# The order of the value products in one attention step: all four column tiles together, or two and two

## The chip, the cores and the metric

The kernel runs on one core of one Trainium2 chip. The metric is the device time of one execution in microseconds (us). The kernel before took 3443.28 us, the median of three runs (3435.34, 3443.28 and 3454.9 us).

A core has five engines that run their own instruction streams side by side: TensorE (PE in the profile; its weight loads are shown apart as PEld), VectorE (DVE), ScalarE (ACT), GpSimd (POOL) and SyncE (SP). A product on TensorE has a held operand, which is loaded into the array first, and a moving operand, which is streamed through it. A held operand of 32 columns fills only one of four *column tiles* of the array, called tile 0 to tile 3 here. Which tile it is follows from the 32 output partitions that the product writes: 0-31, 32-63, 64-95 or 96-127.

## What is computed

Sixteen graphs of 1024 nodes with 256 features each pass through two graph layers. Layer 0 is attention with 4 heads of 64 features; layer 1, which this change touches, is attention with 8 heads of 32 features and then an MLP of width 1024. Cut to what matters here, layer 1 is:

```python
normed = layer_norm(x, gamma1, beta1)
qkv = normed.reshape(b_, n_, H, HD).transpose(0, 2, 1, 3)        # H = 8, HD = 32
scores = jnp.einsum('bhqd,bhkd->bhqk', qkv, qkv) * scale
masked = jnp.where(adj_matrix[:, None] > 0, scores, -jnp.inf)
attn = jax.nn.softmax(masked, axis=-1)
out = jnp.einsum('bhqk,bhkd->bhqd', attn, qkv)
x = x + out
...
return x + gelu(layer_norm(x, gamma2, beta2) @ W1 + b1) @ W2 + b2
```

The kernel takes the softmax as exponentials times a 0/1 mask. It sums masked weight times value, and also the masked weights alone, and divides one by the other at the end.

## The kernel before

**Two streams.** Layer 0 of one graph is interleaved with layer 1 of the graph before it. `layer0` (L955) and `layer1` (L973) are generators; the loop at L1023 picks which of them emits its next piece. It picks by a model of the engines' times, `Pace` (L90, with its costs in `cost`, L123, and its due times in `enter`, L151). The order on each engine is the order of emission. The last graph's layer 1 has no layer 0 beside it.

**A step of layer 1.** `attention1` (L722) walks through 32 steps for a graph: 2 halves of 512 queries, 2 groups ("quads") of 4 heads, and 8 blocks of 128 keys. That makes 512 steps in all. In iteration i it emits

- `exponentials` (L740) of step i: four score products on TensorE (`ps<-nT` in the profile, 32 rows each) into four PSUM tiles, and four exponentials on ScalarE into two tiles `p` of two heads each, called ps[0] and ps[1];
- `masked` (L758) of step i-1: two multiplications by the mask on VectorE, ps[0] first and then ps[1] (`p<-p,mask`);
- `products` (L762) of step i-3, since `LAG` is 3 (L782). These are the subject of the change.

**The products of a step.** All write to PSUM and add up over the 8 key blocks.

- *Moved* products, four of them. The two heads of ps[0] are streamed, 512 queries at a time, against held values of 32 columns (`po<-p,v`: "values", tiles 0 and 1). They are streamed again against a held tile whose first column is one (`unit`, L249; `po<-p,unit`: "ones", tiles 2 and 3), which gives the sums of the weights. All four write one PSUM tile, `moved`.
- *Held* pieces, 32 of them. Of the two heads of ps[1], pieces of 32 queries are the held operand and the values with a column of ones (33 columns) are streamed (`po<-v,p`). For each head and each of four blocks of 128 queries, the four pieces go to tiles 0, 1, 2, 3. They write another PSUM tile, `held`.

Operands are float32, and TensorE runs each product as two passes. In the built program the passes of a product stand one after the other, each with its weight load. So a step has 8 moved passes and 64 held passes: two moved passes and 16 held passes on every tile.

Before the change the order is: values on tile 0, ones on tile 2, values on tile 1, ones on tile 3, and then the 32 held pieces with the tile as the innermost loop.

**What comes after.** At the last key block of a quad, `heads_out` (L815) takes over: ScalarE copies `moved` (`oT<-po`), VectorE divides `held` by its sums, TensorE transposes the copy (`acc<-ident,oT`), and VectorE divides that too. After the four quads the MLP follows (`mlp`, L872; `ps<-yT,w_sb` and `po<-w_sb,hid`). Layer 0's attention gives TensorE the groups `acc<-v,p` (L567, L588), and its preparation (L484) gives the groups `acc<-w0e,xT`, `acc<-identb,ak` and `acc<-ident,xk`. All engine instructions that go through `Pace` stand in the profile under line 61, so groups are told apart by their tiles.

Of the kernel before, what the change touches and what calls it, by code (L numbers as in the profile page):

```python
# [39 lines left out]
P = 128  # L40
# [136 lines left out]
def fast_path(  # L177
# [24 lines left out]
    nc = Pace(tc.nc)  # L202
# [5 lines left out]
    HD = D // H1  # L208
    NB = N // P
# [4 lines left out]
    BPH = HALF // P  # L214
    Q = 32
    TILE = 64
    AHEAD = 3
    PAIR = 2
    GB = 2
    QUAD = 4  # L220
# [28 lines left out]
    unit = const.tile([P, Q], F32, name="unit")  # L249
# [26 lines left out]
    at = one.tile([P, 3, PAIR, HO, T], F32, name="v0")  # L276
# [93 lines left out]
    def bank0(shape, dtype=F32):  # L370
        i = min((i for i in range(2) if not banks0[i]["busy"]), key=lambda i: banks0[i]["taken"])
        for chain in banks0[i]["readers"]:
            complete(chain)
        banks0[i].update(readers=[], taken=1 + max(bank["taken"] for bank in banks0))
        return ps_a.tile(shape, dtype, f"acc{i}"), banks0[i]
# [55 lines left out]
    def begin(chain, engine, *needs):  # L431
        for n in needs:
            if not callable(n):
                uses(chain, n.tensor.name)
        chains.append([chain, engine, needs])
# [10 lines left out]
    def advance():  # L446
        for _ in range(2):
            for item in list(chains):
                if item in chains and when(item[2]) <= max(nc.now(), nc.free[item[1]]):
                    run(item)  # L450
# [271 lines left out]
    def attention1(half, mask, rinv, half_done):  # L722

        steps = [(n, quad, jb) for n in range(NH) for quad in range(H1 // QUAD) for jb in range(NB)]

        turn = [0]

        def logits_tile():

            turn[0] = (turn[0] + 1) % 6
            if place[0][0] == B and turn[0] >= QUAD:
                return bank0([P, HALF])[0]
            return ps_s.tile([P, HALF], F32, name="ps")

        def exponentials(n, quad, jb):  # L740
            keys = slice(jb % BPH * P, (jb % BPH + 1) * P)
            of_keys, of_queries = half(jb // BPH)[2], half(n)[2]
            tiles = [logits_tile() for _ in range(QUAD)]

            nc.together(tiles)
            for e in range(QUAD):
                q = slice(e * HD, (e + 1) * HD)
                nc.tensor.matmul(tiles[e], of_keys[q, quad, keys], of_queries[q, quad, :], start=True, stop=True)
            nc.together(tiles)
            ps = []  # L750
            for e in range(0, QUAD, PAIR):
                p = eight.tile([P, PAIR, HALF], F32, name="p")
                for i in range(PAIR):
                    nc.scalar.activation(p[:, i, :], tiles[e + i], AF.Exp, scale=SCALE1)
                ps.append(p)
            return ps

        def masked(n, quad, jb, ps):  # L758
            for p in ps:
                nc.vector.tensor_mul(p, p, mask[n][:, jb, None, :].to_broadcast([P, PAIR, HALF]))  # L760

        def products(quad, jb, ps, moved, held):  # L762
            values = half(jb // BPH)[1][:, jb % BPH, :, :]
            for e in range(PAIR):
                hd = quad * QUAD + e
                for at, v in ((e, values[:, hd, 0:HD]), (PAIR + e, unit)):
                    nc.tensor.matmul(
                        moved[at * Q : (at + 1) * Q, :], v, ps[0][:, e, :], start=jb == 0, stop=jb == NB - 1
                    )
            for e in range(PAIR):  # L770
                hd = quad * QUAD + PAIR + e
                for q in range(BPH):
                    for at in range(0, P, Q):
                        nc.tensor.matmul(
                            held[at : at + Q, q, e, :],
                            ps[1][:, e, q * P + at : q * P + at + Q],
                            values[:, hd, :],
                            start=jb == 0 and e == 0 and q == 0,
                            stop=jb == NB - 1 and e == PAIR - 1 and q == BPH - 1,
                        )  # L780

        LAG = 3  # L782
        ready = {}

        def logits_ready():
            return ps_s.ready("ps", QUAD)

        def outs_ready():
            return ps_o.ready("po", 2)

        for i in range(len(steps) + LAG):
            if i < len(steps):
                ready[i] = exponentials(*steps[i])
                advance()
            if 0 <= i - 1 < len(steps):
                masked(*steps[i - 1], ready[i - 1])
                advance()
            if i < LAG:
                yield 1.0, logits_ready
                continue  # L800
            n, quad, jb = steps[i - LAG]
            if jb == 0:
                moved = ps_o.tile([P, HALF], F32, name="po")
                held = ps_o.tile([P, BPH, PAIR, HD + 1], F32, name="po")
            products(quad, jb, ready.pop(i - LAG), moved, held)
            if jb == NB - 1:
                if quad == 0:
                    o = one.tile([P, BPH, D], F32, name="o0")
                chain = heads_out(n, quad, moved, held, o, rinv)
                begin(chain, "vector", held, moved, o)  # L810
                if quad == H1 // QUAD - 1:
                    half_done(n, o, chain)
            yield (2.5, logits_ready, *ready.get(i - LAG + 1, ()), *([outs_ready] if jb == NB - 1 else []))

    def heads_out(n, quad, moved, held, o, rinv):  # L815

        oT = two.tile([P, HALF], F32, name="oT1")
        nc.scalar.copy(oT, moved)
        of_heads = o.rearrange("p k (h e) -> p k h e", e=HD)
        rinv = rinv[:, n * BPH : (n + 1) * BPH, :]  # L820

        def divide(first, sums, src):
            heads = slice(quad * QUAD + first, quad * QUAD + first + PAIR)
            nc.vector.reciprocal(rinv[:, :, heads], sums)
            nc.vector.tensor_mul(
                of_heads[:, :, heads, :], src, rinv[:, :, heads][:, :, :, None].to_broadcast([P, BPH, PAIR, HD])
            )

        yield "vector", held
        divide(PAIR, held[:, :, :, HD], held[:, :, :, 0:HD])  # L830
        yield "tensor", oT, side_ready
        pt = side_bank([P, BPH, QUAD, Q])
        for q in range(BPH):
            nc.tensor.transpose(
                pt[:, q, :, :].rearrange("p e z -> p (e z)"), oT[:, q * P : (q + 1) * P], ident
            )
        yield "vector", pt
        divide(0, pt[:, :, PAIR:, 0], pt[:, :, 0:PAIR, :])
# [650 lines left out]
```

## Time and profile before

| what | value |
|---|---|
| runs | 3435.34, 3443.28, 3454.9 us; median 3443.28 us |
| profiled execution | span 3453.7 us from the first to the last instruction; it is 1.2 us under the slowest of the three runs, and no other time is listed for it |
| mean granted TensorE clock | 0.980 |
| TensorE (PE) busy | 3312.8 us, 96% of the span |
| weight loads (PEld) busy | 2252.1 us, 65% |
| VectorE (DVE) busy | 2981.3 us, 86% |
| ScalarE (ACT) busy | 1935.6 us, 56% |
| GpSimd (POOL) busy | 418.6 us, 12% |
| moved passes, mean of one | 615 ns (2048 with values, 2048 with ones) |
| held passes, mean of one | 199 ns (32768) |
| mask product of one p tile | 1217 ns (1024) |

How to read it: "busy" is the time in which at least one instruction of the engine was under way. TensorE's products are pipelined. A pass is recorded from its start to a modelled end, and the next may start long before that end, also on the same tile. So the distance between starts tells what a pass costs, not its duration. One graph takes some 210 us: about 110 us of layer 1's attention and about 90 us of its MLP, both mixed with layer 0 of the next graph.

### The profile page before, as it was taken

The numbers are of one execution on the slowest core, as the hardware profiler recorded it, in microseconds if no ns is written. First come the engines' busy times: TensorE is split into PE (matmuls) and PEld (weight loads), VectorE is DVE, ScalarE is ACT, GpSimd is POOL, SyncE is SP. The second block draws the span as 40 slices with busy tenths as digits, with TensorE's granted clock in tenths as the row PEclk, the third lists the DMA queues.
The fourth block names the chain that finished last, engine by engine and source line by source line (L and its number), as shares of the span: only waits on it lengthen the run. The fifth ranks groups of instructions, "written<-read, shape, count | busy, mean of one in ns | idle before, by whom it ended". The sixth has DMA issues, their size and how long they took to land.

```text
span 3453.7 us, 141035 instructions
## 1 busy us (share of the span) xinstructions
PE 3312.8 (96%) x64161; PEld 2252.1 (65%) x64161; DVE 2981.3 (86%) x5262; ACT 1935.6 (56%) x4192; POOL 418.6 (12%) x424
## 2 busy tenths in 40 slices
PE   5899999999999999999999999999999999999998
PEld 4558576675856758576585766757667585775846
DVE  5898898988979898898988989889898898989883
ACT  2563846547375573746637466473654737556373
POOL 1102011010110101101020110101101011010200
PEclk9899999999999999999999999999999999999999
DMA  5211202011020111202112020120201102010000
GB/s 135 51 22 40 44 27 57 15 44 40 28 59 21 42 34 34 56 19 59 22 38 46 24 57 19 41 43 26 59 15 46 38 28 62 18 44 23 23 6 15
DMA packets 95728, 131.30 MB, mean 38 GB/s; under 512 B 10385, under 2 KB 61585, under 8 KB 95121
## 3 DMA queue, kind: packets, MB, share of 16 engines
q1 hardware_dynamic: 75104, 87.58, 8.2%
q0 software_dynamic: 18432, 33.56, 6.6%
q8 instruction: 504, 8.26, 1.0%
q10 hardware_dynamic: 1584, 1.05, 0.1%
q14 instruction: 104, 0.84, 0.1%
HBM read 138.68 MB, written 17.04 MB: 45 GB/s over the span
## 4 chain that ended last, share of the span: by engine, by line
PE 72%; DVE 20%; ACT 5%; issue 2%; DMA 1%; POOL 0%; SPq 0%; POOLq 0%; ACTq 0%; DVEq 0%
PE po L61 28%; PE ps L61 24%; PE acc L61 20%; DVE p L61 15%; ACT p L61 2%; DVE o L61 1%; DVE x L61 1%; ACT sq L61 1%; DVE st L61 1%; DVE z L61 1%; ACT mask L61 1%; ACT hb L61 1%; DVE v L61 0%; ACT z L61 0%; DVE hb L61 0%
## 5 line engine op out<-in xcount | busy, mean ns | idle before, releaser
L61 ACT ACTIVATE p<-ps 128x512 f32<-128x512 f32 x2006 | 1042.2, 616 | 384.1 <-PE ps L61 341.5
L61 DVE TENSOR_TENSOR p<-p,mask 128x1024 f32<-128x1024 f32 x1024 | 1186.6, 1217 | 6.8 <-ACT p L61 6.8
L61 DVE SCALAR_TENSOR_TENSOR p<-cb,dinv,mask 128x512 f32<-128x512 f32 x1024 | 711.0, 744 | 0.1
L61 ACT ACTIVATE hid<-ps,b_sb 128x256 f32<-128x256 f32 x512 | 242.0, 473 | 795.0 <-PE ps L61 794.7
L61 PE MATMUL ps<-nT 32*128 32x512 f32 x4012 | 676.3, 655 | 0.0
L61 PEld LDWEIGHTS po<-v,p 128*32 128x32 f32 x32768 | 396.1, 110 | 333.2 <-issue 288.5
L61 PE MATMUL acc<-v,p 128*64 128x65 f32 x16384 | 562.2, 226 | 31.0 <-DVE p L61 14.3
L61 PEld LDWEIGHTS acc<-v,p 128*64 128x64 f32 x16384 | 515.2, 140 | 112.9 <-issue 59.0
L61 PE MATMUL po<-p,v 128*32 128x512 f32 x2048 | 552.9, 615 | 0.0
L61 PE MATMUL po<-p,unit 128*32 128x512 f32 x2048 | 552.7, 615 | 0.0
L61 PE MATMUL ps<-yT,w_sb 128*128 128x256 f32 x2048 | 489.8, 385 | 0.0
L61 PE MATMUL po<-w_sb,hid 128*128 128x256 f32 x2048 | 474.6, 384 | 0.0
L61 PEld LDWEIGHTS po<-w_sb,hid 128*128 128x128 f32 x2048 | 381.7, 190 | 54.5
L61 PEld LDWEIGHTS ps<-yT,w_sb 128*128 128x128 f32 x2048 | 375.5, 190 | 51.5
L61 PE MATMUL po<-v,p 128*32 128x33 f32 x32768 | 391.4, 199 | 12.4 <-issue 8.5
L61 PEld LDWEIGHTS po<-p,v 128*32 128x32 f32 x2048 | 78.5, 109 | 332.9 <-issue 174.7
L61 PEld LDWEIGHTS ps<-nT 32*128 32x128 f32 x4012 | 220.1, 186 | 98.0 <-issue 41.3
L61 POOL TENSOR_TENSOR r<-v,mhalf 128x1 f32<-128x1 f32 (+1 forms) x192 | 157.6, 831 | 705.7 <-DVE v L61 623.8
L61 DVE TENSOR_TENSOR z<-acc,bias_r 128x256 f32<-128x256 f32 x128 | 54.1, 423 | 181.7 <-ACT hb L61 181.4
L61 PE MATMUL acc<-w0e,xT 128*128 128x264 f32 x512 | 154.1, 425 | 37.2 <-DVE z L61 22.9
L61 POOL DMA_DIRECT2D ak<-in_adj_dram x128 | 69.7, 545 | 971.5 <-PE acc L61 959.0
L61 POOL TENSOR_TENSOR r<-v1s,mhalf 128x4 f32<-128x4 f32 x32 | 61.5, 1922 | 981.1 <-DVE v1s L61 981.1
(111 smaller groups left out, 2818.5 us busy)
## 6 DMA issues: line engine op xcount, KB each, us to landing
ak<-in_adj_dram POOLq DMA_DIRECT2D x128, 256.0 KB, 3.9
cb<-esr SPq DMA_DIRECT2D x64, 512.0 KB
xk<-in_x_dram SPq DMA_DIRECT2D x64, 256.0 KB
xl<-in_x_dram SPq DMA_DIRECT2D x32, 512.0 KB
out_dram<-z SPq DMA_DIRECT2D x128, 128.0 KB
w_sb<-in_L_gnn_W_dram SPq DMA_DIRECT2D x2, 1024.0 KB
esr<-rows SPq DMA_DIRECT2D x64, 4.0 KB
v<-in_L_gnn_a_src_dram SPq DMA_DIRECT2D x2, 320.0 KB
```

The costliest lines, as they stand in the source:

```text
L61: return method(*args, **kwargs)
```

## The change

The two *values* products come first, on tiles 0 and 1. Behind them are the 16 held pieces that belong to tiles 2 and 3. Then come the two *ones* products on tiles 2 and 3, and behind them the 16 held pieces that belong to tiles 0 and 1. The products themselves, their operands, their tiles and their number stay the same. The weight that a held piece adds first (`start`) and last (`stop`) is told by e, q and the key block as before, tile by tile.

```diff
         def products(quad, jb, ps, moved, held):
             values = half(jb // BPH)[1][:, jb % BPH, :, :]
+
+            def move(group, v, e):
+                nc.tensor.matmul(
+                    moved[group * Q : (group + 1) * Q, :], v, ps[0][:, e, :], start=jb == 0, stop=jb == NB - 1
+                )
+
+            def hold(groups):
+                for e in range(PAIR):
+                    hd = quad * QUAD + PAIR + e
+                    for q in range(BPH):
+                        for at in (group * Q for group in groups):
+                            nc.tensor.matmul(
+                                held[at : at + Q, q, e, :],
+                                ps[1][:, e, q * P + at : q * P + at + Q],
+                                values[:, hd, :],
+                                start=jb == 0 and e == 0 and q == 0,
+                                stop=jb == NB - 1 and e == PAIR - 1 and q == BPH - 1,
+                            )
+
             for e in range(PAIR):
-                hd = quad * QUAD + e
-                for at, v in ((e, values[:, hd, 0:HD]), (PAIR + e, unit)):
-                    nc.tensor.matmul(
-                        moved[at * Q : (at + 1) * Q, :], v, ps[0][:, e, :], start=jb == 0, stop=jb == NB - 1
-                    )
+                move(e, values[:, quad * QUAD + e, 0:HD], e)
+            hold((PAIR, PAIR + 1))
             for e in range(PAIR):
-                hd = quad * QUAD + PAIR + e
-                for q in range(BPH):
-                    for at in range(0, P, Q):
-                        nc.tensor.matmul(
...
-                        )
+                move(PAIR + e, unit, e)
+            hold((0, 1))
```

The planner is told of the same products in another order, and it re-plans a little. In the built program, in each of 15 graphs, one set of transposes `acc<-ident,oT` stands ahead of a group of score products instead of behind it. In the MLP's stretch a few groups of `acc<-v,p` and `ps<-yT,w_sb` that stood apart are joined (304 runs of `acc<-v,p` become 289, and 219 runs of `ps<-yT,w_sb` become 204). VectorE's and ScalarE's instructions are the same, with a few neighbours changed in place.

More of the change, by code (lines that the diff above doesn't have):

```diff
@@ L763, in products @@
             values = half(jb // BPH)[1][:, jb % BPH, :, :]
-            for e in range(PAIR):
-                hd = quad * QUAD + e
-                for at, v in ((e, values[:, hd, 0:HD]), (PAIR + e, unit)):
-                    nc.tensor.matmul(
-                        moved[at * Q : (at + 1) * Q, :], v, ps[0][:, e, :], start=jb == 0, stop=jb == NB - 1
-                    )
-            for e in range(PAIR):
-                hd = quad * QUAD + PAIR + e
-                for q in range(BPH):
-                    for at in range(0, P, Q):
-                        nc.tensor.matmul(
[L775 to L779, printed above, removed]
-                        )
+            def move(group, v, e):
[14 more added lines that the diff above has]
+                            )
+            for e in range(PAIR):
+                move(e, values[:, quad * QUAD + e, 0:HD], e)
+            hold((PAIR, PAIR + 1))
+            for e in range(PAIR):
+                move(PAIR + e, unit, e)
+            hold((0, 1))
         LAG = 3
```

## The prediction

> **What bounds the kernel now.** I read the page's busy shares and then its chain of work that ended last. TensorE leads:
>
> ```profile
> PE 3312.8 (96%) x64161; PEld 2252.1 (65%) x64161; DVE 2981.3 (86%) x5262; ACT 1935.6 (56%) x4192; POOL 418.6 (12%) x424
> ...
> PE 72%; DVE 20%; ACT 5%; issue 2%; DMA 1%; POOL 0%; SPq 0%; POOLq 0%; ACTq 0%; DVEq 0%
> ```
>
> The averages mix stages, so I next cut one graph's 210 us into stretches. The columns are the stretch, its length, busy us (and instructions) of PE, PEld, DVE, ACT, POOL, then clock, DMA share and GB/s.
>
> ```profile
> 985.00:1035.00 50.00, 49.92 (x1246) 26.06 (x1244) 38.63 (x44) 41.16 (x95) 2.65 (x5) 1.00 0.33 67
> 1035.00:1085.00 50.00, 48.13 (x1354) 26.83 (x1346) 49.52 (x69) 32.86 (x68) 2.46 (x2) 1.00 0.05 9
> 1085.00:1175.00 90.00, 90.00 (x1289) 77.30 (x1290) 79.13 (x170) 31.39 (x62) 17.36 (x14) 1.00 0.12 34
> ```
>
> The first stretch holds steps 0-15 of layer 1's attention: PE is full and VectorE has 11 us to spare. The second holds steps 16-31: VectorE is busy for 49.5 of 50 us, so a faster PE finds nobody to feed it. The third is the MLP, PE's alone. So PE time saved in steps 0-15 counts, and in steps 16-31 hardly.
>
> Then I read two neighbouring steps' products in PE's timeline (start, length, what, count of passes):
>
> ```profile
> 1500.73 0.62 PE L61 MATMUL po<-p,v 128*32 128x512 f32 x1
> 1500.73 0.62 PE L61 MATMUL po<-p,unit 128*32 128x512 f32 x1
> 1500.74 0.62 PE L61 MATMUL po<-p,v 128*32 128x512 f32 x1
> 1500.75 0.62 PE L61 MATMUL po<-p,unit 128*32 128x512 f32 x1
> 1501.18 0.59 PE L61 MATMUL po<-p,v 128*32 128x512 f32 x1
> ...
> 1501.61 0.73 PE L61 MATMUL po<-v,p 128*32 128x33 f32 x63
> 1502.14 0.59 PE L61 MATMUL po<-p,v 128*32 128x512 f32 x1
> 1502.16 0.20 PE L61 MATMUL po<-v,p 128*32 128x33 f32 x1
> 1502.16 0.61 PE L61 MATMUL po<-p,v 128*32 128x512 f32 x1
> 1502.18 0.61 PE L61 MATMUL po<-p,unit 128*32 128x512 f32 x2
> ```
>
> The four first moved passes start together, the four second passes 0.45 us later, the held pieces 0.43 us after that, and these last some 0.55 us. The median of 512 steps, from the first moved start: second pass 453 ns, first held pass 883, last held pass 1432, next group of products 1559 ns.
>
> **What a tile can give.** If a held pass costs its tile a fixed time, reordering gains nothing; if the four tiles get in each other's way, it gains. The records show both. In the median step the first 24 held starts come in fours every 31-33 ns; from about the 28th on they come in twos every 16.6 ns, which is 33.2 ns per tile. The whole run is 549 ns for 63 steps of the count, 34.9 ns per pass of a tile. The floor is a tile's own. `acc<-v,p` streams 65 columns on two wider tiles and repeats every 58.3 ns per tile, and a second moved pass of 512 columns takes 430 ns. Through these two, a pass costs 0.832 ns per column and about 4 ns more; for 33 columns that is 31.5 ns, just what the first fours show. So of 34.9 ns only 3.4 ns are the crowd's. With two tiles at a time one held pass is needed every 15.8 ns, where the crowded phase delivers one every 8.3 ns, so I take the floor.
>
> **The sum for one step.** Before, every tile has 883 ns of moved passes and 16 held passes; the last starts at 1432 and streams until 1432 + 31.5 = 1463 ns. After, tiles 0 and 1 do values until 883 ns and then 16 x 31.5 = 504 ns of held passes: 1387 ns. Tiles 2 and 3 do held passes first, to about 504 + 20 (the first pass after another tiling takes 453, not 430) = 524 ns, then 2 x 430 of ones: 1384 ns. The work of a tile is the same and the tiles stay balanced: the gain is 1463 - 1387 = **0.075 us per step**, the crowd's share and no more. Its two ends, were nothing else in play, are 0 (the 34.9 ns stay) and 0.075.
>
> This needs PE to let held pieces pass the values' waiting second passes. The trace bears on it. The passes of a product stand one behind the other in the program, yet at 1500.73-1500.75 four first passes start ahead of any second. At 1502.14 the next step's values start before the last held record at 1502.16, and both values ahead of both ones, although a ones product stands between them; so it is in 26 of the 512 steps. A pass whose tile is taken doesn't hold up another tile's. But it is some six passes that overtake here; after the change it is 32.
>
> [...]
>
> **On the path.** Batches here are graphs.
> - Steps 0-15 of 15 graphs: 240 x 0.075 = 18.0 us gained. The last graph runs without layer 0, PE-bound (a step every 2.63 us): 32 x 0.075 = 2.4 us.
> - Steps 16-31 of 15 graphs: up to 240 x 0.075 = 18.0 us, which I take as 0. VectorE's stretch is full and ends the stage; it only begins earlier by what steps 0-15 gain.
> - The plan: 15 pairs of neighbouring groups are joined in the PE-bound MLP. A group of 64 `acc<-v,p` records takes 2.02 us on the chain, one of 96 takes 2.95, so 32 records are 0.93 and 0.16 is fixed; eight passes of `ps<-yT` take 1.92 or 1.73 us, so up to 0.19 is fixed. 15 x 0.35 = 5 us gained (0 to 5). The moved transposes wait for the copy `oT`, which in that place ends 2.59 us after the step's first product, about when PE gets there (1.56 + 1.09 us): 0.
> - `moved` is complete some 0.5 us later. Its copy is ScalarE's (56% busy) and needed by PE 0.95 us or more after its end, where it isn't already waited for. Where it is (two places of a graph, copies held by ScalarE's own queue at 3.2-3.3 us): 0. `p` tiles come free at the same step's end: the exponentials that reuse them wait for score products that stand behind: 0.
>
> **The wait that moves.** Held pieces read ps[1], whose mask product ends 1.14 us after that of ps[0]. Before, they start 0.88 us into the step; now at its beginning, and the ones products queue behind the waiting instruction. Median slack is 3.9 us, but in 36 steps ps[1] is late:
>
> ```profile
> 1712.84 2.35 DVE L61 TENSOR_TENSOR p<-p,mask 128x1024 f32<-128x1024 f32 x2
> ...
> 1714.11 0.62 PE L61 MATMUL po<-p,v 128*32 128x512 f32 x1
> ...
> 1715.24 0.66 PEld L61 LDWEIGHTS po<-v,p 128*32 128x32 f32 x64 [0.98 <-DVE p L61]
> ```
>
> The mask product ends at 1715.19, 1.08 us after the values start. Before, 0.55 us of held pieces follow it; after, 0.50 of pieces and 0.86 of ones. The cost of such a step is its lateness plus 0.055, at most 0.883 us. Over the 22 cases in steps 30 and 31, right ahead of the PE-bound MLP, that sums to 13.3 us, which I count. The 14 cases in step 23 (5.8 us) lie in VectorE's stretch: hidden, 5.8 us if not.
>
> Sum: -18.0 - 2.4 - 5 + 13.3 = **-12 us** against the profiled execution's 3453.7 (0.35%): 3441.6. On the runs' median 3443.28, 0.3% under that execution, it is 3431 us.
>
> **Rivals.**
> 1. *It overlaps, and the late waits are absorbed or steps 16-31 gain as well.* For it: PE waits little there (1.6 us of a graph). Against it: VectorE's 49.5 of 50. At the most 38.4 + 5 = 43 us: 3400. This is the forecast's own far end.
> 2. *Nothing comes of it.* The pieces overlap but stream beside long passes at the crowded 34.9 ns, or slow them by as much (430 to 453 ns as after another tiling): gain 0, and all late waits count, 19 us, and 512 x 0.022 = 11 us more: 3443 to 3473. For it: no row shows long and short passes side by side for more than 0.02 us.
> 3. *Slower: a waiting pass holds the queue.* If the window in which PE looks ahead is too short for 32 held passes, those on tiles 2 and 3 start only behind the values' second passes, at 453 ns. They end at 957, ones at 1818, held pieces on 0 and 1 behind the ones' second start, 1387 + 504 = 1891 ns: 0.43 us more than before. Steps 0-15 and the last graph: 272 x 0.43 = 117 us; steps 16-31: 6.9 us a graph less the 1.6 that PE waits anyway, 15 x 5.3 = 80. Some 3640 us. It decides once pieces on tiles 2 and 3 start at 0.45 us instead of about 0.01. Against it: the overtaking above; for it: only six passes were seen to overtake. A half-blocked window lies between.
>
> **How the numbers follow.** Overlap works (forecast and rival 1): 0.68, 3400 to 3450; rival 2: 0.14; rival 3: 0.18. A measurement of this kernel can tell about 0.5% (17 us) from no change. Faster by more, below 3426: under half of the first case, 0.30. Slower by more, above 3460: rival 3 and a part of rival 2, 0.23. Within: 0.47. The range takes the first two cases, 0.82, with a few us for the spread of the runs: 3396 to 3474.
>
> **What would show it.** Right: held passes on tiles 2 and 3 from 0.01 us on, ones at about 0.52, pieces for tiles 0 and 1 at 0.88, a next group at 1.48 instead of 1.56 us, and a step 31 that ends later. Wrong: held pieces that begin at 0.45 us; second passes later than 0.45; or a gain in steps 16-31.

## The result, and the profile after

The changed kernel takes 3757.41 us (median of four runs, 3756.65 to 3759.48) beside 3445.15 us for the kernel before (median of four, 3435.34 to 3454.9). The ratio is 1.0917, 95% interval 1.0895 to 1.0939: slower by 312 us. The profiled execution has a span of 3754.9 us, 301 us more than that of before, whose profiled execution (3453.7) lies at the upper end of its runs.

From the page after, the busy shares and the chain of work that ended last:

```profile
PE 3630.2 (97%) x64161; PEld 2511.8 (67%) x64161; DVE 2992.6 (80%) x5262; ACT 1948.0 (52%) x4192; POOL 422.2 (11%) x424
...
PE 84%; issue 8%; ACT 5%; DVE 3%; DMA 1%; POOL 0%; SPq 0%; POOLq 0%; ACTq 0%; DVEq 0%
PE po L61 37%; PE ps L61 26%; PE acc L61 21%; ACT p L61 1%; DVE p L61 1%; ACT sq L61 1%; ACT mask L61 1%; ACT oT L61 0%; ACT z L61 0%; ACT hb L61 0%; DVE z L61 0%; DMA w0e<-in_L_gnn_W_dram 0%; DVE hb L61 0%; POOL r L61 0%; ACT yT L61 0%
```

The counts of instructions are as before. PE's busy time grew by 317 us, VectorE's by 11. On the chain VectorE fell from 20% to 3%: it is no longer the one waited for, even in the stretch that it filled before. The line to read is `po`, the products of a step: 37% of 3754.9 us.

The timeline of PE after, one step (start, length, what, count of passes that start one after another):

```profile
843.07 0.62 PE L61 MATMUL po<-p,v 128*32 128x512 f32 x2
843.09 0.63 PE L61 MATMUL po<-v,p 128*32 128x33 f32 x27
843.53 0.59 PE L61 MATMUL po<-p,v 128*32 128x512 f32 x1
843.53 0.19 PE L61 MATMUL po<-v,p 128*32 128x33 f32 x1
843.53 0.59 PE L61 MATMUL po<-p,v 128*32 128x512 f32 x1
843.72 0.65 PE L61 MATMUL po<-v,p 128*32 128x33 f32 x3
844.17 0.61 PE L61 MATMUL po<-p,unit 128*32 128x512 f32 x1
844.20 0.23 PE L61 MATMUL po<-v,p 128*32 128x33 f32 x3
844.24 0.59 PE L61 MATMUL po<-p,unit 128*32 128x512 f32 x1
844.25 0.54 PE L61 MATMUL po<-v,p 128*32 128x33 f32 x23
844.62 0.59 PE L61 MATMUL po<-p,unit 128*32 128x512 f32 x1
844.62 0.23 PE L61 MATMUL po<-v,p 128*32 128x33 f32 x3
844.67 0.59 PE L61 MATMUL po<-p,unit 128*32 128x512 f32 x1
844.81 0.69 PE L61 MATMUL po<-v,p 128*32 128x33 f32 x4
845.42 0.94 PE L61 MATMUL acc<-w0e,xT 128*128 128x264 f32 x3
```

The overlap is there: 28 held passes start in the first 0.46 us, beside the values. Then it stops. One more comes at 0.65 (843.72), two more at 1.07 us, and only then the first ones product (844.17). The same is seen again behind the ones: 3, 23 and 3 passes, then one at 1.74 us (844.81) and the last ones from 2.17 us on. Over 512 steps the median start of the last held pass is 2226 ns (1432 before) and that of the next group 2353 ns (1559): **0.794 us more per step**.

Three stretches of a graph after, which answer to the three shown of before: steps 0-15, steps 16-31, MLP (columns as there).

```profile
1060.00:1120.00 60.00, 59.62 (x1238) 33.75 (x1236) 40.28 (x46) 40.73 (x94) 2.65 (x5) 1.00 0.23 51
1123.00:1180.00 57.00, 56.47 (x1378) 33.82 (x1381) 49.84 (x68) 30.50 (x63) 1.94 (x1) 1.00 0.05 13
1185.00:1275.00 90.00, 89.67 (x1139) 76.34 (x1137) 79.11 (x183) 33.04 (x71) 20.14 (x18) 1.00 0.12 34
```

In the second stretch VectorE has about as much work as before (49.8 us, then 49.5), but now in 57 us instead of 50. PE binds it.

By the starts of the steps' products in the two traces, a mean over 15 graphs (the last row is one graph):

| stretch | before, us | after, us | more | 0.794 us of each step would be |
|---|---|---|---|---|
| step 0 to step 16 | 58.19 | 68.70 | 10.5 | 12.7 |
| step 16 to step 31 | 47.90 | 56.68 | 8.8 | 11.9 |
| step 31 to the next graph's step 0 | 104.19 | 103.59 | -0.6 | 0.8 |
| last graph, step 0 to step 31 | 95.7 | 115.2 | 19.5 | 24.6 |

15 x (10.5 + 8.8 - 0.6) + 19.5 = 300 us: all of the 301 us between the spans. Of 512 x 0.794 = 406 us a quarter didn't arrive; it replaced waits that PE had before. The score products (`ps<-nT`), for one, are busy for 624.1 us after and 676.3 before, with the same 4012 recorded passes.

### The profile page after: what moved, and what is told of

It reads as the page before. It is cut to its first block, busy times and chain, and to the rows that moved or that the text cites. A ratio compares the mean times of both kernels' runs of the same rounds, so it can differ in the third digit from the quotient of the medians.

```text
span 3754.9 us, 141050 instructions
## 1 busy us (share of the span) xinstructions
PE 3630.2 (97%) x64161; PEld 2511.8 (67%) x64161; DVE 2992.6 (80%) x5262; ACT 1948.0 (52%) x4192; POOL 422.2 (11%) x424
## 4 chain that ended last, share of the span: by engine, by line
PE 84%; issue 8%; ACT 5%; DVE 3%; DMA 1%; POOL 0%; SPq 0%; POOLq 0%; ACTq 0%; DVEq 0%
PE po L61 37%; PE ps L61 26%; PE acc L61 21%; ACT p L61 1%; DVE p L61 1%; ACT sq L61 1%; ACT mask L61 1%; ACT oT L61 0%; ACT z L61 0%; ACT hb L61 0%; DVE z L61 0%; DMA w0e<-in_L_gnn_W_dram 0%; DVE hb L61 0%; POOL r L61 0%; ACT yT L61 0%
## 5 line engine op out<-in xcount | busy, mean ns | idle before, releaser
L61 PEld LDWEIGHTS po<-v,p 128*32 128x32 f32 x32768 | 768.8, 111 | 411.3 <-issue 334.6
L61 PE MATMUL po<-v,p 128*32 128x33 f32 x32768 | 986.6, 197 | 9.9
L61 PE MATMUL ps<-nT 32*128 32x512 f32 x4012 | 624.1, 654 | 0.0
L61 PE MATMUL acc<-v,p 128*64 128x65 f32 x16384 | 556.5, 226 | 22.8 <-DVE p L61 13.3
L61 PE MATMUL po<-p,v 128*32 128x512 f32 x2048 | 542.6, 608 | 0.0
L61 PEld LDWEIGHTS ps<-nT 32*128 32x128 f32 x4012 | 181.8, 186 | 88.4 <-issue 48.4
```

Of the source, the lines that this page charges most:

```text
L61: return method(*args, **kwargs)
```

## The experiments

**The theory, W (window).** The stop comes after a number of instructions, not at a time: behind the 28th held pass, which starts at 0.454 us in the median step and at 0.754 us in one with a granted clock of 0.50 (below). A float32 product is four instructions: load, pass, load, pass (the trace has 2048 passes and 2048 loads of the 1024 values products). Count from the first values pass as place 1. The second pass of that product is place 3, the other values product ends at place 7, and the n-th held pass is at place 7 + 2n. The 28th, the last before the stop, is at place 63; the 29th at 65. My reading of this, which the runs below try: *in these kernels TensorE looks at 64 instructions, starts any whose tile is free, but makes room only in program order and only when an instruction is complete.* The trace shows the starts; its ends are modelled, so the completion is part of the reading. In the median step the tile of the first values pass starts its second pass at 0.453 us. Exactly one more held pass (two places) starts 0.19 us later, at 0.643 us, which W takes for the completion of the first. Of the second values pass that makes 0.453 + 0.43 + 0.19 = 1.073 us; the 30th held pass starts at 1.072, and the rest behind it. The loads fit the count in the same trace: in the median step the load of the 29th held pass, place 64, starts at 0.449 us, and that of the 30th, place 66, only at 0.647. Every pass here has just one load, so 32 passes and one load ahead of them would look the same; no kernel below tells the two apart.

**The rivals.** S (second pass): the start of a moved product's second pass stops short passes elsewhere; it comes at 0.453 us, just where the stop is. G (gear change): each change between moved and held products costs its own drain, and the change made three of them out of one.

**Three tiles beside one values product** tells the count from the time:

```diff
-            for e in range(PAIR):
-                move(e, values[:, quad * QUAD + e, 0:HD], e)
-            hold((PAIR, PAIR + 1))
-            for e in range(PAIR):
-                move(PAIR + e, unit, e)
-            hold((0, 1))
+            value(0)
+            hold((1, 2, 3))
+            value(1)
+            ones(0)
+            ones(1)
+            hold((0,))
```

Here `value(e)` is the move with the values of head e, and `ones(e)` the one with the ones tile.

> All products stay; the order is values on tile 0, the 24 held pieces of tiles 1, 2 and 3, values on tile 1, both ones, the 8 held pieces of tile 0. Theory W (window): TensorE looks at some 64 instructions (weight loads and passes) in program order, and an instruction only makes room once all before it are complete, which for a pass is about 0.19 us after its stream. In the changed kernel the 28th held pass stood at place 63 behind the first values pass and was the last to start before the stall. With one values product in front instead of two, the 30th held pass is the one at place 63. Three tiles take a pass every 10.5 ns, so W expects a stop after 30 or so held passes, at about 0.31 us, which is before the second values pass starts (0.45); then one more at 0.64 and the rest from 1.07 us, and the step's last held pass at 1.74 us or a little more. Theory S (second pass): what stops the held pieces is the start of a second moved pass, as in my third rival and as the stop at 0.45 us in the changed kernel suggests; then held pieces go on until 0.45 us, some 43 passes, and stop there. Time of the whole kernel: W some 0.08 us under the changed kernel's step in the model, but the values on tile 1 come late; 3700 to 3760 us.

Measured: 3747.35 us (one execution; 3453.85 us before, median of 11 in this job). One step in PE's timeline of this kernel:

```profile
1106.04 0.62 PE L61 MATMUL po<-p,v 128*32 128x512 f32 x1
1106.05 0.52 PE L61 MATMUL po<-v,p 128*32 128x33 f32 x30
1106.49 0.59 PE L61 MATMUL po<-p,v 128*32 128x512 f32 x1
1106.68 0.81 PE L61 MATMUL po<-v,p 128*32 128x33 f32 x17
1107.30 0.59 PE L61 MATMUL po<-p,v 128*32 128x512 f32 x1
```

Thirty held passes, the last at 0.330 us in the median step, and then nothing until 0.643 us, although the second values pass starts only at 0.453. The next ones come at 0.643 (one), 1.073, 1.081; the last at 1.759 us. W holds to the pass; S, which wanted some 43 passes until 0.45, falls.

The trace of the changed kernel holds the same test. The first gap of over 100 ns between two held starts comes behind the 28th in all of its 512 steps, and four of these lie in stretches where the granted clock was 0.50 to 0.59. One of them (clock 0.50):

```profile
367.18 1.07 PE L61 MATMUL po<-p,v 128*32 128x512 f32 x2
367.20 0.99 PE L61 MATMUL po<-v,p 128*32 128x33 f32 x28
368.04 1.07 PE L61 MATMUL po<-p,v 128*32 128x512 f32 x2
368.27 1.12 PE L61 MATMUL po<-v,p 128*32 128x33 f32 x3
```

The 28th held pass starts at 0.754 us and the 29th at 1.088, though the second values passes start only at 0.854. The times have moved, the count has not.

**Twelve or fourteen pieces in front of the ones** moves the last instruction of the ones across place 64. `hold` here takes a range of the eight rounds of its tiles. The kernel with fourteen has 7 in both places of the 6:

```diff
             value(0)
             value(1)
-            hold((2, 3))
+            hold((2, 3), 0, 6)
             ones(0)
             ones(1)
             hold((0, 1))
+            hold((2, 3), 6)
```

> All products stay; as the change, but only 12 of the 16 held pieces of tiles 2 and 3 stand between values and ones, the other four at the end of the step. Theory W (window of 64, room made in program order on completion): values 8 instructions, 12 pieces 48, ones 8: all 64 fit, the last ones pass is at place 63 behind the first values pass. The ones start at about 0.38 us, their second passes at 0.81, held pieces for tiles 0 and 1 at 1.07 when the values are complete, the last held pass at about 1.57 us: 0.14 us more than before the change (1.43) and 0.66 less than the change (2.23). The kernel: some 3480 to 3530 us. Theory S (a second moved pass stops held pieces): the ones' second passes would stop the held pieces again; the ones start at 0.38, the last held pass comes at about 1.9 us or later. Theory G (each change between moved and held costs its own drain of some 0.6 us): as in the change, about 2.2 us and 3750.

> All products stay; as e2_twelve with 14 held pieces instead of 12 between values and ones, the other two at the end. Theory W: 8 + 56 + 8 instructions are 72; the first ones product's first pass is at place 65 and can start only when the first values pass is complete, 0.64 us, and the second ones product's first pass when that product is complete, 1.07 us; the last held pass comes at about 2.19 us and the kernel takes about as long as the changed one, 3730 to 3760 us. Theories S and G see no difference that matters between 12 and 14 pieces: ones at about 0.44 us, and a step within 0.1 us of e2_twelve's.

Measured: 3517.41 us with twelve, 3761.01 us with fourteen, one execution each. PE's timeline with twelve:

```profile
1022.77 0.62 PE L61 MATMUL po<-p,v 128*32 128x512 f32 x2
1022.79 0.57 PE L61 MATMUL po<-v,p 128*32 128x33 f32 x24
1023.19 0.60 PE L61 MATMUL po<-p,unit 128*32 128x512 f32 x2
1023.23 0.60 PE L61 MATMUL po<-p,v 128*32 128x512 f32 x2
1023.62 0.60 PE L61 MATMUL po<-p,unit 128*32 128x512 f32 x2
1023.66 0.94 PE L61 MATMUL po<-v,p 128*32 128x33 f32 x40
```

and with fourteen:

```profile
1081.81 0.62 PE L61 MATMUL po<-p,v 128*32 128x512 f32 x2
1081.82 0.63 PE L61 MATMUL po<-v,p 128*32 128x33 f32 x27
1082.26 0.59 PE L61 MATMUL po<-p,v 128*32 128x512 f32 x1
1082.26 0.20 PE L61 MATMUL po<-v,p 128*32 128x33 f32 x1
1082.27 0.59 PE L61 MATMUL po<-p,v 128*32 128x512 f32 x1
1082.45 1.05 PE L61 MATMUL po<-p,unit 128*32 128x512 f32 x3
1082.91 0.63 PE L61 MATMUL po<-v,p 128*32 128x33 f32 x27
1083.34 0.59 PE L61 MATMUL po<-p,unit 128*32 128x512 f32 x1
```

With twelve, both ones products start right behind the pieces (0.418 us) and run on; the last held pass of the step starts at 1.623, the next group at 1.749 us. With fourteen, the two ones products start at 0.644 and 1.082 us, the times that W takes for the completion of the first and the second pass of the first values product, and the step ends as in the change (2.228, next group 2.355). Two pieces more in front cost 0.6 us of a step and 244 us of the kernel. S and G saw no difference between them; both fall. Nor is it the planner: on TensorE the other groups come in the same order in both kernels and in the changed one. Twelve still cost 0.19 us of a step against the old order, since the pieces of tiles 0 and 1 lie past place 64: all but the first start only from 1.07 us on, though their tiles are free at 0.88 (0.453 + 0.43).

**The same order with half the instructions.** In bfloat16 a product is one pass (2 + 16 + 2 + 16 of them in the step below), a step 72 instructions. Both orders, each changed in the same way:

```diff
-    unit = const.tile([P, Q], F32, name="unit")
+    unit = const.tile([P, Q], BF16, name="unit")
...
-                p = eight.tile([P, PAIR, HALF], F32, name="p")
+                p = eight.tile([P, PAIR, HALF], BF16, name="p")
...
-        v1 = two.tile([P, BPH, H1, HD + 1], F32, name="v1")
+        v1 = two.tile([P, BPH, H1, HD + 1], BF16, name="v1")
```

> The order from before the change, with the masked weights p, the layer-1 values and the ones tile of the products in bfloat16 instead of float32 (the sums stay in float32), so that a product is one pass instead of two: a changed computation, whose time counts only beside the next kernel's. A step has 72 instructions instead of 144. Theory W (window of 64): moved passes at 0, held passes when they end, some 0.24 us if a pass of 512 columns takes half of the 430 ns; 28 of 32 held passes are within the window, so the last starts at 0.40 to 0.50 us.

> The changed order with the same bfloat16 operands (a changed computation as in the run before). Values 4, held pieces 32, ones 4 instructions: 40 fit into 64, and so do 12 of the last 16 held passes. Theory W: nothing stalls between the values and the ones; ones at about 0.15 us, the last held pass at 0.40 to 0.55 us, the step within 0.08 us of the old order's and the kernel within 1% of it, where in float32 the new order costs 0.79 us of a step and 9%. Theory G (each change between moved and held products costs its own drain, 0.2 to 0.6 us, whatever the number of instructions): the step is 0.4 us or more longer than the old order's and the kernel some 5%. Theory S (a second pass stops short ones): there are no second passes here, no difference, as W.

Measured: 3358.85 us in the old order and 3358.03 us in the new, one execution each. TensorE is on 58% and 56% of their chains, so the step tells more than the kernel's time. A step of the new order in PE's timeline:

```profile
1019.65 0.40 PE L61 MATMUL po<-p,v 128*32 128x512 bf16 x2
1019.65 0.37 PE L61 MATMUL po<-v,p 128*32 128x33 bf16 x16
1019.87 0.38 PE L61 MATMUL po<-p,unit 128*32 128x512 bf16 x2
1019.88 0.41 PE L61 MATMUL po<-v,p 128*32 128x33 bf16 x16
```

Values with 16 held passes beside them, ones with the other 16, and no stop between. The next group starts at 571 ns in the median step, 573 in the old order. So three turns between moved and held products cost the step no more here than one does (G falls again). In both orders the last four held passes start from 0.417 us on, 0.19 us after 0.227, when the tile of the first moved pass starts its next one: by W's count 28 held passes fit behind the moved ones in the old order, and 12 of the last 16 in the new. The ones came at 0.226 us, not at 0.15: held passes on two tiles took 25 ns per tile.

**Held pieces first.** If a long pass should not stand in front of many short ones, put the short ones first (against the order before the change, written with the same helpers):

```diff
+            hold(range(4))
             for e in range(PAIR):
                 value(e)
                 ones(e)
-            hold(range(4))
```

> All products stay; the 32 held pieces come first, the tile innermost as before the change, then values, ones, values, ones. Theory W: no long pass is in front of many short ones, so nothing stalls: the moved products start at about 0.50 to 0.53 us, their second passes at 0.93 to 0.97, the next group of products at about 1.49 us instead of 1.56 (before the change held pieces are slowed once their first 25 or so have used up the window). That is 0.07 us of a step; 272 steps outside VectorE's full stretch give 19 us, and the wait for ps[1], which now stands at the head of the step, takes some 13 us back: 3425 to 3450 us against 3445, the same or a little faster. Theory S agrees on the step's order of events here. Theory G (each change between moved and held costs a drain): one change as before, step as before, and the wait makes it slower: 3445 to 3465.

Measured: 3479.86 us beside 3453.85, ratio 1.0079 (1.0059 to 1.0100). Nothing stalls, as W has it: moved products start at 0.55 to 0.60 us, their second passes at 0.99 to 1.04. But the next group starts at 1.559 us, as before the change, and the kernel is 26 us slower. The gain of 0.07 us isn't there: the held passes slow down in this order too, with no long pass ahead of them. They come in fours up to the 32nd, then unevenly, and one every 8.3 ns from about the 42nd on. Before the change the fours ended with the 24th. Both are place 63: before, 8 moved passes and their loads take the first 16 places; here, none. Moreover the second four begins some 24 ns later than before, and the tiles end 50 ns apart.

For the 26 us I took the wait for ps[1], now at the head of the step, to be the cause (theory L): the stretch from step 16 to 31 takes 49.24 us instead of 47.90 between the first moved passes of the two steps (48.98 between the first passes of any kind). Two kernels tried it, together with a third that splits the held pieces. In the first, VectorE masks ps[1] ahead of ps[0]:

```diff
-            for p in ps:
+            for p in reversed(ps):
                 nc.vector.tensor_mul(p, p, mask[n][:, jb, None, :].to_broadcast([P, PAIR, HALF]))
```

> All products stay; as e4_held_first, but VectorE multiplies ps[1], which the held pieces read, by the mask before ps[0]. Theory L (the late mask product costs e4_held_first its 26 us: its step is as long as before the change, 1.56 us, but the stretch of steps 16-31 takes 1.3 us a graph more, because a step can only begin when ps[1] is masked, the later of the two): the step then begins at the earlier mask product again; where VectorE is late the moved products wait instead, with 0.86 us behind them instead of 0.55, so a graph is some 0.3 to 0.5 us longer than before the change: 3450 to 3465 us beside 3454 of before and 3480 of e4_held_first. If the 26 us have another cause (the plan, or the copies of the moved sums that end later), it stays at 3470 to 3485.

In the second, the last two steps of a graph keep the order from before the change:

```diff
+            if n == NH - 1 and quad == H1 // QUAD - 1 and jb >= NB - 2:
+                for e in range(PAIR):
+                    value(e)
+                    ones(e)
+                hold(range(4))
+                return
             hold(range(4))
```

> All products stay; as e4_held_first, but the last two of a graph's 32 steps keep the order from before the change. Theory L: the two steps, in which VectorE has just masked ps[0] and still works on ps[1], carry the cost of e4_held_first; with them in the old order the stretch of steps 16-31 takes 48 us again instead of 49.2 and the kernel 3450 to 3460 us beside 3454. If the cost is spread over other steps: 3470 to 3480.

In the third, that too, and in the other steps 20 held pieces ahead of the moved products and 12 behind:

```diff
-            hold(range(4))
+            hold(range(4), 0, 5)
             for e in range(PAIR):
                 value(e)
                 ones(e)
+            hold(range(4), 5)
```

> All products stay; 20 held pieces (five rounds of the four tiles), then the four moved products, then the other 12 held pieces; the last two steps of a graph keep the order from before the change. Theory W (window of 64 instructions): moved 16 instructions and 12 pieces 48 just fit, so the 24 held passes behind the moved ones are all at hand when these end and run at a tile's own 31.5 ns. Moved products start at about 0.34 us, their second passes at 0.78, the last held pass at 1.38 to 1.40 and the next group of products at 1.51 to 1.53 us instead of 1.56. Where VectorE has time to spare (272 steps) that is 8 to 14 us; the wait for ps[1] at the head of the step takes a part of it back: 3440 to 3455 us beside 3454. If the slow second half of the held pieces before the change is not the window's doing but the rate at which TensorE gets instructions, nothing is gained: next group at 1.55 or later, 3455 to 3470.

Measured, beside 3448.7 us of before: ps[1] masked first 3478.96 us, ratio 1.0093 (1.0068 to 1.0118); last two steps in the old order 3473.67 us, 1.0071 (1.0046 to 1.0096); 20 and 12 pieces 3453.79 us, 1.0013 (0.9997 to 1.0030).

L falls as the cause of the whole. From the first pass of step 16 to the first pass of step 31 these kernels take 48.98 us with held pieces first, 48.79 with ps[1] masked first and 48.65 with the last two steps in the old order, beside 47.90 before the change: neither edit gives back more than a third of the 1.08 us. With the last two steps in the old order another 0.77 us of a graph are lost before step 16. (Between first moved passes that kernel shows 48.09 us, which looks like a cure; but in step 16 the first moved pass comes 0.55 us into the step, and in step 31 at its start.) What makes up the 20 to 30 us stays open. In these kernels the 89 groups `acc<-identb,ak` that follow a step start later than before the change, by 76, 129 and 26 ns in the median; that would be some 7, 11 and 2 us, an estimate that no run tried. The planner's order of the other groups on TensorE is the same, group by group, in the three kernels tried after held pieces first, so it doesn't explain the 20 to 25 us by which the third is faster than the other two. The split order, with the step's next group at 1.547 us (1.559 before, 1.51 to 1.53 expected), can't be told from the kernel before: W says rightly that nothing stalls, but the 12 ns that it gains on the median step are too few to show. No version with the same computation beats the kernel before.

## Why the prediction was wrong

**The step that failed** is "This needs PE to let held pieces pass the values' waiting second passes", on which the prediction put 0.68, together with the sum that rests on it: 1463 - 1387, 0.075 us gained per step. Held pieces do pass, 28 of 32, and after a first gap of 53 ns at 31.8 ns per tile, where the prediction had 31.5 from `acc<-v,p` and the moved passes. The sum counted only the time of the tiles. It left out any limit on how far passes overtake. Four held passes, the ones products and all that follow lay past place 64, and all of them but one held pass started only from 1.07 us on. This comes twice in a step: 2 x (1.07 + 0.03) us instead of 1.39. The term of -0.075 us measured +0.794. None of the prediction's three signs of being wrong shows this: held pieces begin at 0.01 us, the values' second passes at 0.45, and steps 16-31 gain nothing. What shows it is a sign of being right that is missing: the ones start at 1.10 us instead of 0.52.

**The third rival** supposed the kind of limit that the runs agree with (how many instructions behind a waiting pass may overtake it) and priced it too low: 0.43 us of a step beside the 0.794 measured. It had the pieces on tiles 2 and 3 start at 0.45 us, and held a window that lets some of them through for a milder case "between". The opposite is so. 28 held passes get through, the last of them at place 63, and the ones products then start not with the second values pass (0.453 us) but at 1.10 us, behind 1.073, where W puts its completion. The rival's time, 3640 us, lies nearer to 3757 than the forecast, 3431; the prediction gave it 0.18.

**The evidence at hand.** The prediction saw six passes overtake and asked for 32, and said so; it took the step from six to 32 as likely. The trace of before held more. In its median step the 24 held passes that came in fours end at 1.07 us after the step's start, where W puts the completion of the second passes. The prediction read the change of pace there as the crowd's, four tiles in each other's way. But the 24th stands at place 63 behind the first moved pass, and with held pieces first the pace changes behind the 32nd, which stands at place 63 there. So in these two kernels the change of pace goes with the 64 places. It isn't a wait for a long pass, since held pieces first have none ahead of them in the step; what sets the later pace of 8.3 ns no run shows.

**What held.**
- VectorE's stretch. A gain in steps 16-31 was taken to be nothing; a loss there is another matter. It came through for 8.8 of 11.9 us, since PE, which comes later, no longer waits for VectorE there (it is busy for 56.47 of 57 us, before for 48.13 of 50) and is the bound itself.
- The wait that moves (13.3 us) was not paid. In steps 30 and 31 the mask product of ps[1] ended 0.0 us before and 0.8 us after the step's start before the change, and 3.2 us before it after: PE is too late to meet it. The term holds only if PE gets faster.
- The plan's 5 us can't be told from the rest: the part from step 31 to the next graph is 0.6 us shorter, 9 us in all, though it holds a step that is 0.79 us longer and other differences.

## What to carry to other kernels

In these kernels small products on free tiles do overtake a long one on TensorE, but not without limit: 28 held passes started beside the two values products, 30 beside one. Both times the last stood at place 63 from the first values pass, and what lay past it started at 0.643 us (one pass) and from 1.07 us on, on whatever tile it was. A float32 product counted four places. Before short products are put beside a long one, count the instructions that stand behind it, and look in a trace whether those past place 64 wait there too. And a term that rests on "these overlap" should be tried at the size at which they must, since an overlap of six says little about one of 32.

## What the runs showed of the hardware that was not expected

- Passes on different column tiles start out of program order: in 460 of the changed kernel's 512 steps 27 held passes start ahead of the second values pass that stands in front of them. How far this goes fits a count of 64 instructions, weight loads included (or 32 passes, each with its load): in five kernels (the change, three tiles, fourteen pieces, and both in bfloat16) the pass at place 63 starts as soon as its turn on its tile comes, and the one at place 65 waits. It starts 0.643 us after the first float32 pass (0.644 with fourteen pieces), whose tile took its next pass after 0.453, and 0.417 us after the first bfloat16 pass, whose tile took its next after 0.227: 0.19 us later in both. With three tiles 30 held passes have started by 0.330 us, yet only one more starts before 1.073. This fits places that come free in program order and on completion; completion itself no view shows.
- Held passes of 33 float32 columns cost their tile 31 to 32.3 ns up to that place, whether two, three or four tiles are at work (31.8 on two in the change, 31.0 on four before it). Behind it (the 24th held pass before the change, the 32nd with held pieces first) four tiles soon get one every 8.3 ns, with or without long passes ahead of them. Passes of 33 bfloat16 columns on two tiles take 25 ns per tile, not half of 31.5.
